# Layer 1's 256x256 products by Strassen's scheme: seven 128x128 block products for two channels and two batches in place of eight

## Chip, cores, metric

The kernel runs on one core of one Trainium2 chip. The metric is device time in microseconds of one execution (with one core, that core's time). A core has five engines that run their own instruction queues [...]: TensorE (matrix products into PSUM; the profile calls it PE and its weight loads PEld), VectorE (DVE), ScalarE (ACT), GpSimd (POOL) and SyncE (SP, which issues most DMAs). A queue is written as its engine with a q: ACTq is ScalarE's queue, in which its DMA issues stand between its computing instructions.

## What is computed

Two layers over an input `x` of 4 x 256 x 256 x 64 (batch, height, width, channel), all in fp32. Layer 0 is a block of layer norm, a Fourier mixing of the plane, a depthwise 3x3 convolution and pointwise products. Layer 1, which this change is about, works along the height alone:

```python
def _L1_conv_ref(x, w_real, w_imag):
    trend = _moving_average(x, KERNEL)
    seasonal = x - trend
    xf = jnp.fft.rfft(seasonal, axis=1)
    xs = xf[:, :M]
    W = w_real + 1j * w_imag
    ys = jnp.einsum('bmnc,cmk->bknc', xs, W)
    ...
    filt = jnp.fft.irfft(yf, n=T, axis=1)
    return trend + filt
```

For a fixed channel all of this is linear in the column of 256 heights, so it is one 256x256 matrix per channel. Layer 1 is then 64 products of a 256x256 matrix with 256 columns for each of 4 batches.

## The kernel before

**Stages.** The kernel builds the 64 matrices of layer 1 early and keeps them in device memory (`m_d`). Layer 0 runs in a long pipeline whose order is written out by hand as lists of operations with due periods, and leaves its result in device memory too (`x2_d`), arranged so that eight channels (CG) of one batch are one contiguous row of 8 KB per partition. Its last lines run until about 3872 us of the span. Then comes layer 1, the last stage, which this change rewrites; nothing else of the kernel is in it.

**Order.** TensorE, VectorE, ScalarE and GpSimd execute in the order in which the program writes their instructions (`in_order`); SyncE's DMAs are placed by the scheduler. Tiles come from pools with a number of buffers for each tag; a new tile waits until all readers of the buffer's earlier tile are done. A DMA also waits for the DMA that used its completion semaphore before; there are eight such semaphores, dealt out in turn to SyncE's and ScalarE's DMAs together.

**Layer 1's loop.** The loop over `c` takes eight channels at a time, the inner loop over `b0` two batches (BH) at a time. `matrix_load` brings the matrices of two channels (CM) as `mt`, 128 partitions x 2 channels x 2 contraction halves `t` x 256 outputs, 512 KB, with eight buffers, that is two groups of eight channels. `x2_load` brings `xc`, the operand of eight channels and two batches, by four DMAs of 1 MB, with one buffer in pool `seq` (the first tile) and three in `seq2`.

**`layer1`.** For each channel and each output half `to` it takes a PSUM bank and issues two matmuls that accumulate over the contraction halves `t`, each with a 128x128 block of `mt` as the weights and 512 columns (two batches x 256) of `xc` as the moving operand. In the trace one such fp32 matmul is two records with a weight load each. The result is evicted with the bias `b_fp[c]`, by VectorE for `to` = 0 (L1518) and by ScalarE for `to` = 1 (L1516), into `oc`, which holds two channels and both batches and has two buffers. When two channels are done, four DMAs of 256 KB, issued by ScalarE (L1523), bring `oc` to the output.

**Banks.** `bank` gives PSUM banks in a ring. Two of the eight banks are given up before layer 0's convolution (`give_back`), which needs them in a pool of its own, and layer 1 keeps to the other six.

Of the kernel before, what the change touches and what calls it, by code (L numbers as in the profile page):

```python
# [11 lines left out]
F32 = mybir.dt.float32  # L12
I32 = mybir.dt.int32
AF = mybir.ActivationFunctionType
ALU = mybir.AluOpType
AX = mybir.AxisListType
PSUM = bass.MemoryType.PSUM
DRAM = bass.MemoryType.DRAM

P = 128  # L20
N = 256
C = 64
# [4 lines left out]
BANKS = 6  # L27
# [109 lines left out]
def conv_seq_kernel(ctx: ExitStack, tc: tile.TileContext, a: dict, tables: bass.AP, out: bass.AP):  # L137
    nc = tc.nc
    x = a["x"]
    B = x.shape[0]  # L140

    consts = ctx.enter_context(tc.tile_pool(name="consts", bufs=1))
    psum = ctx.enter_context(tc.tile_pool(name="psum", bufs=1, space=PSUM))
# [4 lines left out]
    free_banks, taken, lent, busy = list(range(8)), {}, ExitStack(), []  # L148
    pulling = []
    RELEASES = dict(  # L150
        x="xs", m0="b0", m1="b1", z="zs", w="zt", u="uc", s="r1", t0="tt0", t1="tt1", gm="cf0",
# [3 lines left out]
    NEEDS = dict(m0=2, m1=2, u=2, s=2, gm=2, em=2)  # L155
    psum2 = lent.enter_context(tc.tile_pool(name="psum2", bufs=1, space=PSUM))

    def bank(name, keep=True):

        at = free_banks.pop(0)  # L160
        if keep:
            taken[name] = at, busy[-1]
        else:
            free_banks.append(at)
        pool = psum if at < BANKS else psum2
        return pool.tile([P, 512], F32, tag=f"bank{at}", name=name)

    def make_room(op):
# [19 lines left out]
    lent_back = []  # L188

    def give_back():  # L190
        lent_back.append(True)
        for at in range(BANKS, 8):
            if at in free_banks:
                free_banks.remove(at)
# [4 lines left out]
    def row(ap):  # L199
        return ap.rearrange("(o n) -> o n", o=1)  # L200

    def const(shape, name):
        return consts.tile(shape, F32, tag=name, name=name)
# [3 lines left out]
    SW, CG = 16, 8  # L207
# [204 lines left out]
    def prepare(prep):  # L412
# [49 lines left out]
        nc.vector.tensor_copy(w_tegT, ps[:, :C])  # L462
        yield
        ps = bank("ps_wp", False)
        for k in range(2):
            nc.tensor.matmul(
# [1005 lines left out]
        return ops | {"hv": first_half, "hc": between_half, "hm": second_half, "ht": third_half}  # L1472


    CM, CO = 2, 2
    BH = max(1, B // 2)

    b_fp = const([P, C], "b_fp")

    def x2_load(pool, c, b0, bufs):  # L1480
        xc = pool.tile([P, 2, BH, N // SW, CG, SW], F32, tag="xc", name=f"xc_{c}_{b0}", bufs=bufs)
        for b in range(BH):
            for t in range(2):
                nc.sync.dma_start(
                    xc[:, t, b], x2_d[b0 + b, t * P : (t + 1) * P, c // CG]
                )
        return xc

    def matrix_load(pool, c):
        mt = pool.tile([P, CM, 2, N], F32, tag="mt", name=f"mt_{c}", bufs=8)  # L1490
        nc.sync.dma_start(mt, m_d[c : c + CM].rearrange("c p t n -> p c t n"))
        return mt

    def layer1(c, b0, mts, xc, pool):

        nf = BH * N
        oc = None
        for i in range(CG):
            if i % CO == 0:
                oc = pool.tile([P, 2, BH, CO, N], F32, tag="oc", name=f"oc_{c + i}_{b0}", bufs=2)  # L1500
            for to in range(2):
                ps = bank(f"ps_o_{c + i}_{to}_{b0}", False)
                for t in range(2):
                    nc.tensor.matmul(  # L1504
                        ps[:, :nf],
                        mts[i // CM][:, i % CM, t, to * P : (to + 1) * P],
                        xc[:, t, :, :, i, :],
                        start=t == 0,
                        stop=t == 1,
                    )  # L1510
                dst = oc[:, to, :, i % CO, :]
                src = ps[:, :nf].rearrange("p (b n) -> p b n", n=N)

                bias = b_fp[:, c + i : c + i + 1]
                if to:
                    nc.scalar.activation(dst, src, AF.Identity, bias=bias)  # L1516
                else:
                    nc.vector.tensor_scalar(dst, src, bias, None, ALU.add)  # L1518
            if i % CO == CO - 1:
                at = c + i + 1 - CO  # L1520
                for to in range(2):
                    for b in range(BH):
                        nc.scalar.dma_start(  # L1523
                            out[b0 + b, to * P : (to + 1) * P, at : at + CO, :], oc[:, to, b]
                        )

    ET = mybir.EngineType  # L1530
    in_order = tc.manual_schedule(engines={ET.PE, ET.DVE, ET.Activation, ET.Pool})
# [4 lines left out]
    def opened(b):  # L1536

        return (KH * (b + 1) + 2) // 2 + 1

    chunk_at, at = {}, 0  # L1540
    for b in range(B):
        at = max(at, S0 + opened(b) + 2 + LATE)
# [136 lines left out]
    def period(n):  # L1679
        if any(n - k in chunk_at for k in range(7)):  # L1680
            names = FULL if n < B * FWD + 4 else MIXED if n < CONV_FROM else CONV
        else:
            names = SPECTRUM
        joint["on"], joint["whole"] = names is FULL, names is SPECTRUM
        for op, at in names:
            base = n
            if op in PAIRS:
                base = 2 * (n - S0)
            elif op in BACK:
                base = n - S0  # L1690
            elif op in HALF_MATRICES:
                base = (n - S0 - HALF_MATRICES[op]) // 2
            do(op, base + at)

    def starting(n, prep):

        for i, (op, at) in enumerate(FIRST):
            do(op, (3 if op in MATRICES else 2) * n + at)
            if n and i == len(FIRST) // 2:
                next(prep, None)  # L1700

    with in_order, ExitStack() as right:
        with (
            tc.tile_pool(name="fwd", bufs=2, side="left") as fwd,
            tc.tile_pool(name="mix", bufs=2, side="left") as mixing,
        ):
            forward = forward_h(fwd)
            load_group, begin, spectrum = spectral(mixing)
            ops |= forward
            do("fl", 0)  # L1710
            with ExitStack() as early:
                pool = early.enter_context(tc.tile_pool(name="matrices", bufs=2, side="right"))
                prep = early.enter_context(tc.tile_pool(name="prep", bufs=1, side="right"))
                ops |= matrices(pool)
                do("fl", 1)
                nc.sync.dma_start(tab, tables[:, :_L0_END])
                pieces = prepare(prep)
                next(pieces)
                nc.sync.dma_start(b_fp, row(a["b_fp"]).to_broadcast([P, C]))
                for n in range(S0 // 2):  # L1720
                    starting(n, pieces)
                for _ in pieces:
                    pass
                do("yt0", FWD - 1)
                do("yt1", FWD - 1)
                load_group(0)
                for k, names in enumerate(BETWEEN, C - BESIDE - len(BETWEEN)):
                    do("v", k)
                    do("vc", k)
                    do("mt", k - 1)  # L1730
                    for op, at in names:
                        do(op, S0 - 1 + at)
                do("mt", C - BESIDE - 1)
                begin(0)
                ops |= spectrum
                early_end = S0 + 4 * BESIDE + 1
                for n in range(S0, early_end):
                    if n == early_end - 3:
                        give_back()
                    period(n)  # L1740
            lent.close()
            conv = right.enter_context(tc.tile_pool(name="conv", bufs=2, side="right"))
            pairs = right.enter_context(tc.tile_pool(name="pairs", bufs=1, space=PSUM))
            ops |= convolution(conv, pairs)
            for n in range(early_end, S0 + LATE + opened(B - 1) + 2):
                period(n)
        with tc.tile_pool(name="seq", bufs=1, side="left", reuse_waits="tile") as seq:
            mts = [matrix_load(seq, c) for c in range(0, CG, CM)]
            xc = x2_load(seq, 0, 0, 1)
            for n in range(S0 + LATE + opened(B - 1) + 2, END):  # L1750
                period(n)
            right.close()
            with tc.tile_pool(name="seq2", bufs=1, side="right", reuse_waits="tile") as seq2:
                for c in range(0, C, CG):
                    if c:
                        mts = [matrix_load(seq, c + i) for i in range(0, CG, CM)]
                    for b0 in range(0, B, BH):
                        if c or b0:
                            xc = x2_load(seq2, c, b0, 3)
                        layer1(c, b0, mts, xc, seq)  # L1760


# [37 lines left out]
```

## Time and profile before

| what | us |
|---|---|
| three runs | 4324.39, 4318.21, 4323.12; median 4323.12 |
| the profiled execution | 4325.4 |
| its span, first to last instruction | 4323.6 |
| first and last matmul of layer 1, start | 3871.2 and 4317.8 |
| TensorE busy with layer 1's matmuls | 443.3 |
| busy over the whole span: TensorE, VectorE, ScalarE, GpSimd | 4158.0, 3453.4, 2961.5, 3163.4 |

The span is cut into 40 equal slices below, a digit for the busy tenths of each, so that layer 1 is the last four and a bit:

```profile
PE   8999999899999999899999999999998899999999
PEld 4544444345555555455555566666665566654444
DVE  6968999779999998899999878888887799962222
ACT  3338998678888887788888777888885466641111
POOL 6869999688888887788888877888887588840000
PEclk9999999989999999999999999999999999999999
DMA  6664555535454544444444443344433544439995
```

In layer 1 TensorE stays at nine tenths, VectorE falls to two, ScalarE to one and GpSimd to none, while the DMA engines are at nine tenths. The share of busy time over the whole span says nothing of this: it is an average over stages with different limits.

### The profile page before, as it was taken

How to read it: one execution, taken by the hardware profiler on the slowest of the kernel's cores; microseconds unless marked ns; L12 is line 12 of the kernel's file. 1: busy time of each engine (PE TensorE's matmuls, PEld its weight loads, DVE VectorE, ACT ScalarE, POOL GpSimd, SP SyncE). 2: the span in 40 equal slices, each digit the busy share in tenths (PEclk: the TensorE clock that was granted, in tenths of full speed). 3: DMA queues.
4: the chain of work that ended last, by engine and by line, in shares of the span. 5: the costliest groups of instructions: out<-in, count | busy, mean ns of one | idle time of the engine just before them, and what ended most of it. 6: DMA issues, size and time to landing. Idle time of an engine off the chain costs nothing.

```text
span 4323.6 us, 67389 instructions
## 1 busy us (share of the span) xinstructions
PE 4158.0 (96%) x22443; PEld 2315.2 (54%) x22443; DVE 3453.4 (80%) x5234; ACT 2961.5 (68%) x5409; POOL 3163.4 (73%) x3156
## 2 busy tenths in 40 slices
PE   8999999899999999899999999999998899999999
PEld 4544444345555555455555566666665566654444
DVE  6968999779999998899999878888887799962222
ACT  3338998678888887788888777888885466641111
POOL 6869999688888887788888877888887588840000
PEclk9999999989999999999999999999999999999999
DMA  6664555535454544444444443344433544439995
GB/s 190 211 190 142 161 161 162 152 98 137 137 137 137 137 137 124 122 122 138 138 138 129 113 109 109 106 112 112 118 98 91 173 113 118 114 108 358 342 343 228
DMA packets 763906, 655.28 MB, mean 152 GB/s; under 512 B 46413, under 2 KB 657695, under 8 KB 755240
## 3 DMA queue, kind: packets, MB, share of 16 engines
q1 hardware_dynamic: 726696, 583.84, 46.5%
q10 hardware_dynamic: 36864, 67.13, 4.1%
q8 instruction: 180, 2.95, 0.3%
q14 instruction: 166, 1.36, 0.1%
HBM read 364.81 MB, written 286.00 MB: 151 GB/s over the span
## 4 chain that ended last, share of the span: by engine, by line
PE 42%; POOL 6%; DVE 4%; DMA 4%; ACT 3%; issue 1%; SPq 1%; ACTq 0%; POOLq 0%; DVEq 0%
PE ps_o L1504 9%; PE ps_h_c L1166 5%; PE ps_p L750 3%; PE ps_s_c L1041 3%; PE ps_h_c L1180 3%; PE ps_f_c L1283 3%; PE ps_hh_c L1166 2%; PE ps_z L805 2%; PE ps_t_c L1088 2%; PE ps_u L856 2%; PE ps_x L725 2%; PE ps_ft_c L1308 2%; DMA out_dram<-oc 1%; PE ps_zt L823 1%; POOL xb L609 1%
## 5 line engine op out<-in xcount | busy, mean ns | idle before, releaser
L770 DVE TENSOR_TENSOR g<-ps_p,g 128x512 f32<-128x512 f32 x1040 | 702.2, 683 | 127.9 <-ACT g L764 109.7
L781 POOL TENSOR_TENSOR g<-g 128x512 f32<-128x512 f32 (+1 forms) x520 | 677.9, 1315 | 98.5 <-ACT g L775 88.8
L775 ACT ACTIVATE g<-g,b_fc 128x1024 f32<-128x1024 f32 (+1 forms) x520 | 598.3, 1151 | 1.5 <-DVE g L770 1.4
L750 PE MATMUL ps_p<-xs,wp 64*128 64x512 f32 (+1 forms) x2080 | 561.1, 615 | 9.9 <-DVE g L770 2.7
L1166 PE MATMUL ps_h_c<-td,wc_main 128*128 128x256 f32 x2048 | 517.1, 391 | 7.3 <-DVE s_c L1234 0.8
L764 ACT COPY g<-ps_p 128x512 f32<-128x512 f32 (+1 forms) x520 | 298.0, 585 | 268.5 <-PE ps_p L750 101.1
L1504 PE MATMUL ps_o<-xc,mt 128*128 128x512 f32 x1024 | 443.3, 595 | 3.9 <-DVE oc L1518 3.8
L1166 PEld LDWEIGHTS ps_h_c<-td,wc_main 128*128 128x128 f32 x2048 | 370.1, 193 | 122.5 <-ACT zt L833 36.7
L1276 ACT ACTIVATE h_c<-h_c,b_conv 128x1024 f32<-128x1024 f32 x256 | 297.6, 1164 | 140.6 <-DVE h_c L1245 54.1
L1518 DVE TENSOR_SCALAR oc<-ps_o,b_fp 128x512 f32<-128x512 f32 x128 | 93.5, 749 | 351.4 <-DMA out_dram<-oc 196.7
L1516 ACT ACTIVATE oc<-ps_o,b_fp 128x512 f32<-128x512 f32 x128 | 86.2, 686 | 363.0 <-PE ps_o L1504 196.7
L1128 POOL TENSOR_TENSOR td<-tt 128x512 f32<-128x512 f32 x256 | 327.0, 1299 | 10.0
L1504 PEld LDWEIGHTS ps_o<-xc,mt 128*128 128x128 f32 x1024 | 195.3, 191 | 251.2 <-issue 236.0
L609 POOL TENSOR_TENSOR xb<-xt 128x512 f32<-128x512 f32 x224 | 285.4, 1282 | 54.5 <-DVE xt L602 41.1
L750 PEld LDWEIGHTS ps_p<-xs,wp 64*128 64x128 f32 x2080 | 189.3, 186 | 239.6 <-issue 84.7
L805 PE MATMUL ps_z<-g,w_tp 128*64 128x512 f32 x1024 | 288.7, 617 | 24.6 <-POOL g L781 19.9
L725 PEld LDWEIGHTS ps_x<-tab,yb 128*64 128x64 f32 x4064 | 235.0, 138 | 133.3 <-issue 69.2
L1322 DVE TENSOR_TENSOR st<-x_c,ps_ft_c 128x256 f32<-128x256 f32 x512 | 261.8, 602 | 44.4 <-PE ps_ft_c L1308 41.4
L615 PE MATMUL ps_y<-xb,tab 128*64 128x512 f32 x1024 | 273.4, 623 | 23.3 <-POOL xb L609 17.1
L1283 PE MATMUL ps_f_c<-h_c,w_fp 128*64 128x512 f32 x1024 | 266.3, 615 | 15.6 <-ACT h_c L1276 15.5
L1180 PE MATMUL ps_h_c<-td,wc_half 64*128 64x256 f32 (+1 forms) x2048 | 278.6, 396 | 2.4 <-POOL td L1132 1.1
L1041 PE MATMUL ps_s_c<-uc_c,tab 64*128 64x512 f32 x1024 | 259.6, 616 | 15.6 <-DVE uc_c L990 8.7
(201 smaller groups left out, 9559.4 us busy)
## 6 DMA issues: line engine op xcount, KB each, us to landing
y_d<-yt SPq DMA_DIRECT2D x256, 256.0 KB, 3.6
yb<-y_d SPq DMA_DIRECT2D x256, 256.0 KB, 4.0
u_d<-ut SPq DMA_DIRECT2D x256, 256.0 KB, 3.6
x_c<-in_x_dram SPq DMA_DIRECT2D x512, 128.0 KB, 3.6
x_d<-st SPq DMA_DIRECT2D x128, 512.0 KB, 5.1
xc<-x_d SPq DMA_DIRECT2D x64, 1024.0 KB, 8.5
out_dram<-oc ACTq DMA_DIRECT2D x256, 256.0 KB, 5.8
xt<-in_x_dram SPq DMA_DIRECT2D x504, 128.0 KB, 2.5
```

Source lines behind the costliest of these rows:

```text
L609: engine.tensor_tensor(sums[j][:, i], x0, x1, (ALU.add, ALU.subtract)[i])
L750: nc.tensor.matmul(ps[:, :nf], wp[rows, cols], rhs[rows], start=True, stop=r == 1 or not pr["special"],)
L770: nc.vector.tensor_tensor(gt[:, i], re, gt[:, 1], op)
L775: nc.scalar.activation(g, g, AF.Gelu, bias=b_fc[:, half : half + 1])
L781: nc.gpsimd.tensor_tensor(g[:, 0], g[:, 0], g[:, 1], op)
L805: nc.tensor.matmul(ps[r * C : (r + 1) * C, :nf], w_tp, d[:, :nf], start=True, stop=True)
L1041: nc.tensor.matmul(pss[i], tb[i * C : (i + 1) * C], uc[i * C : (i + 1) * C, ::-1, 1 - r, :] if down else uc[i * C : (i + 1) * C, :, r, :], ...
L1128: tt_(new[:, k : k + 3 : 2], a_c, nb_e, op)
L1166: nc.tensor.matmul(product(j, k, par), wc_main[:, par, k, :], td[:, k, slots(j)].rearrange("p j q -> p (j q)"), start=k in (0, 1, 3), stop ...
L1180: nc.tensor.matmul(product(j, k, par)[:, dst.start * Q : dst.stop * Q], wc_half[lo : lo + C, k, :], td[lo : lo + C, k, src].rearrange("p j ...
L1283: nc.tensor.matmul(ps[par * C : (par + 1) * C], w_fp, gs[j][:, :, par, i0 : i0 + 2, :].rearrange("p r j q -> p r (j q)"), start=True, stop ...
L1504: nc.tensor.matmul(ps[:, :nf], mts[i // CM][:, i % CM, t, to * P : (to + 1) * P], xc[:, t, :, :, i, :], start=t == 0, stop=t == 1,)
```

## The change

The 256x256 matrix of a channel is seen as four 128x128 blocks (two contraction halves by two output halves), and the operand as four blocks too: two contraction halves by the two batches. The product of two such 2x2 arrangements takes eight block products by the plain rule; Strassen's scheme (in the form with fifteen sums) takes seven, and sums of blocks before and after.

- `matrix_sums`, once per pair of channels: four sums of matrix blocks by VectorE, into `ms`.
- `operand_sums`, once per pair of channels and pair of batches: four sums of operand blocks by GpSimd, into `x_sums`, which has two buffers.
- `layer1` now handles one pair of channels and one pair of batches. It issues seven products, each of two matmuls (one for each channel) of 128x256 that don't accumulate, into a bank of its own. ScalarE writes product 1 with the bias to `oc`; VectorE adds the other products in seven additions, each of which reads a bank and an earlier part of `oc`. ScalarE then issues the four output DMAs as before. `oc` has four buffers.
- The loop runs over 64 such steps. `ahead` writes the sums of the next step in front of the present step's `layer1`.
- `mt` has four buffers in place of eight, and each is loaded again for the channel eight further on. `xc` has three in place of four.
- Layer 1 gets the two missing banks back (`psum3`), so that the ring has eight.

```diff
-    def layer1(c, b0, mts, xc, pool):
-        nf = BH * N
-        oc = None
-        for i in range(CG):
...
-            for to in range(2):
-                ps = bank(f"ps_o_{c + i}_{to}_{b0}", False)
-                for t in range(2):
-                    nc.tensor.matmul(
-                        ps[:, :nf],
-                        mts[i // CM][:, i % CM, t, to * P : (to + 1) * P],
-                        xc[:, t, :, :, i, :],
-                        start=t == 0,
-                        stop=t == 1,
-                    )
...
+    def matrix_sums(c, mt, pool):
+        ms = pool.tile([P, 4, CM, P], F32, tag=f"ms{c % CG}", name=f"ms_{c}", bufs=1)
...
+        tt = nc.vector.tensor_tensor
+        tt(ms[:, 0], a21, a22, ALU.add)
+        tt(ms[:, 1], ms[:, 0], a11, ALU.subtract)
+        tt(ms[:, 2], a11, a21, ALU.subtract)
+        tt(ms[:, 3], a12, ms[:, 1], ALU.subtract)
+        return ms
+    def operand_sums(c, b0, xc, pool):
+        i = c % CG
+        xs = pool.tile([P, 4, N // SW, CM * SW], F32, tag="x_sums", name=f"x_sums_{c}_{b0}", bufs=2)
...
+        tt = nc.gpsimd.tensor_tensor
+        tt(xs[:, 0], b12, b11, ALU.subtract)
+        tt(xs[:, 1], b22, xs[:, 0], ALU.subtract)
+        tt(xs[:, 2], b22, b12, ALU.subtract)
+        tt(xs[:, 3], b21, xs[:, 1], ALU.subtract)
+        return xs
+    def layer1(c, b0, mt, xc, ms, xs, outs):
...
+        def product(k, a, x):
+            ps = bank(f"ps_o_{name}_{k}", False)
+            for ch in range(CM):
+                nc.tensor.matmul(
+                    ps[:, ch * N : (ch + 1) * N], a[:, ch], x[:, ch], start=True, stop=True
+                )
+            return ps
+        oc = outs.tile([P, 2, BH, CM * N], F32, tag="oc", name=f"oc_{name}", bufs=4)
+        add = lambda dst, x, ps: nc.vector.tensor_tensor(dst, x, ps, ALU.add)
+        p1 = product(1, left(0, 0), right_(0, 0))
+        p6 = product(6, ms[:, 1], sums(1))
+        p2 = product(2, left(1, 0), right_(1, 0))
+        p7 = product(7, ms[:, 2], sums(2))
+        p5 = product(5, ms[:, 0], sums(0))
+        p4 = product(4, left(1, 1), sums(3))
+        p3 = product(3, ms[:, 3], right_(1, 1))
+        for ch in range(CM):
+            cols = slice(ch * N, (ch + 1) * N)
+            nc.scalar.activation(
+                oc[:, 0, 0, cols], p1[:, cols], AF.Identity, bias=b_fp[:, c + ch : c + ch + 1]
+            )
+        add(oc[:, 0, 1], oc[:, 0, 0], p6)
+        add(oc[:, 0, 0], oc[:, 0, 0], p2)
+        add(oc[:, 1, 1], oc[:, 0, 1], p7)
+        add(oc[:, 0, 1], oc[:, 0, 1], p5)
+        add(oc[:, 1, 0], oc[:, 1, 1], p4)
+        add(oc[:, 1, 1], oc[:, 1, 1], p5)
+        add(oc[:, 0, 1], oc[:, 0, 1], p3)
+        for to in range(2):
+            for b in range(BH):
+                nc.scalar.dma_start(
+                    out[b0 + b, to * P : (to + 1) * P, c : c + CM, :],
+                    oc[:, to, b].rearrange("p (c n) -> p c n", c=CM),
+                )
...
+                def ahead(k):
+                    c, b0, at = steps[k]
+                    if (c, b0) not in tiles:
+                        left_one = len(tiles) % 3 == 0
+                        tiles[c, b0] = x2_load(seq if left_one else seq2, c, b0, 1 if left_one else 2)
+                    if b0 == 0:
+                        sums[at] = matrix_sums(at, mt_of[at], seq2)
+                    return operand_sums(at, b0, tiles[c, b0], seq2)
+                xs = ahead(0)
+                for k, (c, b0, at) in enumerate(steps):
+                    if b0 == 0 and at + CG < C:
+                        mt_of[at + CG] = matrix_load(seq, at + CG)
+                    then = ahead(k + 1) if k + 1 < len(steps) else None
+                    layer1(at, b0, mt_of[at], tiles[c, b0], sums[at], xs, seq)
+                    xs = then
```

More of the change, by code (lines that the diff above doesn't have):

```diff
@@ L156, in conv_seq_kernel @@
     psum2 = lent.enter_context(tc.tile_pool(name="psum2", bufs=1, space=PSUM))
+    extra = [psum2]
     def bank(name, keep=True):
@@ L164, in bank @@
             free_banks.append(at)
-        pool = psum if at < BANKS else psum2
+        pool = psum if at < BANKS else extra[-1]
         return pool.tile([P, 512], F32, tag=f"bank{at}", name=name)
@@ L1472, in matrices @@
         return ops | {"hv": first_half, "hc": between_half, "hm": second_half, "ht": third_half}
-    CM, CO = 2, 2
-    BH = max(1, B // 2)
+    CM = 2
+    BH = 2
     b_fp = const([P, C], "b_fp")
@@ L1489, in matrix_load @@
     def matrix_load(pool, c):
-        mt = pool.tile([P, CM, 2, N], F32, tag="mt", name=f"mt_{c}", bufs=8)
+        mt = pool.tile([P, CM, 2, N], F32, tag="mt", name=f"mt_{c}", bufs=4)
         nc.sync.dma_start(mt, m_d[c : c + CM].rearrange("c p t n -> p c t n"))
         return mt
-    def layer1(c, b0, mts, xc, pool):
-        nf = BH * N
-        oc = None
-        for i in range(CG):
-            if i % CO == 0:
-                oc = pool.tile([P, 2, BH, CO, N], F32, tag="oc", name=f"oc_{c + i}_{b0}", bufs=2)
-            for to in range(2):
-                ps = bank(f"ps_o_{c + i}_{to}_{b0}", False)
-                for t in range(2):
-                    nc.tensor.matmul(
-                        ps[:, :nf],
-                        mts[i // CM][:, i % CM, t, to * P : (to + 1) * P],
-                        xc[:, t, :, :, i, :],
-                        start=t == 0,
-                        stop=t == 1,
-                    )
[L1511 to L1525, printed above, removed]
@@ new lines, in matrix_sums @@
+    def matrix_sums(c, mt, pool):
+        ms = pool.tile([P, 4, CM, P], F32, tag=f"ms{c % CG}", name=f"ms_{c}", bufs=1)
+        a11, a12, a21, a22 = (
+            mt[:, :, t, to * P : (to + 1) * P] for to in range(2) for t in range(2)
+        )
[8 more added lines that the diff above has]
+        xs = pool.tile([P, 4, N // SW, CM * SW], F32, tag="x_sums", name=f"x_sums_{c}_{b0}", bufs=2)
+        b11, b12, b21, b22 = (
+            xc[:, t, b, :, i : i + CM, :].rearrange("p s c w -> p s (c w)")
+            for t in range(2)
+            for b in range(BH)
+        )
[5 more added lines that the diff above has]
+        return xs
@@ new lines, in layer1 @@
+    def layer1(c, b0, mt, xc, ms, xs, outs):
+        i = c % CG
+        name = f"{c}_{b0}"
+        left = lambda t, to: mt[:, :, t, to * P : (to + 1) * P]
+        right_ = lambda t, b: xc[:, t, b, :, i : i + CM, :].rearrange("p s c w -> p c s w")
+        sums = lambda k: xs[:, k].rearrange("p s (c w) -> p c s w", c=CM)
+        def product(k, a, x):
[18 more added lines that the diff above has]
+                oc[:, 0, 0, cols], p1[:, cols], AF.Identity, bias=b_fp[:, c + ch : c + ch + 1]
+            )
+        add(oc[:, 0, 1], oc[:, 0, 0], p6)
[10 more added lines that the diff above has]
+                    oc[:, to, b].rearrange("p (c n) -> p c n", c=CM),
+                )
@@ L1752, in conv_seq_kernel @@
             right.close()
[L1753 to L1760, printed above, removed]
+            free_banks.extend(range(BANKS, 8))
+            lent_back.clear()
+            with (
+                tc.tile_pool(name="seq2", bufs=1, side="right", reuse_waits="tile") as seq2,
+                tc.tile_pool(name="psum3", bufs=1, space=PSUM) as psum3,
+            ):
+                extra.append(psum3)
+                steps = [
+                    (c, b0, c + i)
+                    for c in range(0, C, CG)
+                    for b0 in range(0, B, BH)
+                    for i in range(0, CG, CM)
+                ]
+                tiles, sums = {(0, 0): xc}, {}
+                mt_of = dict(zip(range(0, CG, CM), mts))
+                def ahead(k):
[13 more added lines that the diff above has]
+                    xs = then
 _INS = {
```

## The prediction

> **What bounds the kernel now.** I read the page first (engine shares, costliest groups), then the chain of waits from 3860 us on, the windows of the last stage, the tile view of `oc`, and a few moments of the timeline for spacings between instructions. Before the last stage the two programs are the same on every engine (the view that lists instruction order, numbers left out, differs only there), so only layer 1, from 3871 us to the end, can change.
>
> ```profile
> L1504 PE MATMUL ps_o<-xc,mt 128*128 128x512 f32 x1024 | 443.3, 595 | 3.9 <-DVE oc L1518 3.8
> L1518 DVE TENSOR_SCALAR oc<-ps_o,b_fp 128x512 f32<-128x512 f32 x128 | 93.5, 749 | 351.4 <-DMA out_dram<-oc 196.7
> L1516 ACT ACTIVATE oc<-ps_o,b_fp 128x512 f32<-128x512 f32 x128 | 86.2, 686 | 363.0 <-PE ps_o L1504 196.7
> ...
> 3950.63 367.81 PE ps_o L1504 x856
> ...
> 3871.00:3932.00 61.00, 57.23 (x129) 25.02 (x128) 11.95 (x19) 9.69 (x15) 0.00 (x0) 0.95 0.97 362
> 3932.00:4262.00 330.00, 329.87 (x769) 145.64 (x768) 70.52 (x98) 64.84 (x97) 0.00 (x0) 1.00 0.90 340
> ...
> L1523 ACTq DMA_DIRECT2D out_dram<-oc x256: 338/448/2072, 3879.3 to 4319.8; - x128
> ```
>
> The chain is one unbroken piece of TensorE for 368 us. In the windows (TensorE, weight loads, VectorE, ScalarE, GpSimd, clock, DMA share, GB/s) TensorE is busy 329.87 of 330 us, VectorE 21%, GpSimd not at all, DMA 0.90 at 340 GB/s. 769 matmul records in 330 us is 0.429 us each; 1024 records and a slow start make the 447 us from 3871.2 to 4318.5. VectorE and ScalarE only evict, and their waits cost nothing because TensorE has six banks to run into.
>
> These lines give the prices of what is added:
>
> ```profile
> 3847.23 1.89 PE L1166 MATMUL ps_h_c<-td,wc_main 128*128 128x256 f32 x8
> ...
> 3847.03 0.68 DVE L1243 SCALAR_TENSOR_TENSOR h_c<-ps_hh_c,s_c 128x512 f32<-128x512 f32 x1
> 3847.63 0.68 DVE L1244 SCALAR_TENSOR_TENSOR h_c<-ps_hh_c,s_c 128x512 f32<-128x512 f32 x1
> ...
> 3844.97 0.69 DVE L1239 TENSOR_TENSOR ps_hh_c<-h_c,ps_hh_c 128x512 f32<-128x512 f32 x1
> 3845.69 0.70 DVE L1240 TENSOR_TENSOR ps_hh_c<-h_c,ps_hh_c 128x512 f32<-128x512 f32 x1
> ...
> 2467.44 0.70 DVE L1240 TENSOR_TENSOR ps_hh_c<-h_c,ps_hh_c 128x512 f32<-128x512 f32 x1
> 2468.24 0.69 DVE L1242 TENSOR_TENSOR h_c<-ps_hh_c,h_c 128x512 f32<-128x512 f32 x1
> ...
> 3842.98 0.65 ACT L1209 COPY s_c<-ps_h_c 128x256 f32<-128x256 f32 x2 [3.78 <-PE ps_h_c L1180]
> 4119.35 1.85 ACTq L1523 DMA_DIRECT2D out_dram<-oc  x4
> L1128 POOL TENSOR_TENSOR td<-tt 128x512 f32<-128x512 f32 x256 | 327.0, 1299 | 10.0
> L582 DVE TENSOR_TENSOR xb<-xt x256: 674/684/1772, 17.3 to 2391.2; 128x512 f32<-128x512 f32 x128
> ```
>
> The reader should look at starts, not durations: a VectorE instruction follows a free predecessor after 0.60 us, one that waits for VectorE's own last result after 0.72, and one with a further wait beside it after 0.80. Four output DMAs hold ScalarE's queue for 1.85 us (0.34, then 0.45 to 0.48 each, plus 0.04 between).
>
> [...] the spacing of 0.60 is what I use for a chain. [...] eight 128x256 records, each with its own full 128x128 load, take 1.89 us, so 0.216 us apart ((1.89 - 0.38)/7), and the load (0.19 us) is hidden. [...]
>
> **The change, part by part.** One step is now two channels and two batches; there are 64.
>
> TensorE: 8 matmuls of 512 columns (16 records x 0.429 = 6.86 us) become 14 of 256 columns (28 records x 0.216 = 6.05 us). If TensorE stayed the bound, 64 x 0.81 = 52 us would be won.
>
> GpSimd: four sums of 128x512 per step, 4 x 1.30 = 5.2 us, into two `x_sums` buffers. It may start step k+2 when TensorE has used `x_sums` of step k, and has over a step of slack; 5.2 lies under the step. Its 32-element runs are not in the trace: between 1.10 (L1124, strided) and 1.68 (L1125), 4.4 to 6.7 us; I take 5.2. All of it hides beside TensorE.
>
> Matrix sums: four VectorE adds of 256 elements, 0.42 each (L1234), about 1.5 us, in 32 of the 64 steps; placed in front of that step's seven adds. The single `mt` set is reloaded after the fourth product of the b0=2 steps and needed two steps later (some 14 us; the present median to landing is 6.9), and `xc` has three buffers with eight steps between free and needed. I cost these at nothing; a late `mt` would stall VectorE, and with it the stage.
>
> VectorE and ScalarE: this is the part that decides. ScalarE writes product 1 plus bias to `oc`, and VectorE's first add reads it. But on ScalarE's queue these two activations stand behind the four output DMAs of the step before, of which the second waits for that step's seventh add. So there is a ring: last add of step k, three DMA issues, two activations, seven adds of step k+1. Nothing in it overlaps the next turn. Its length:
> - VectorE to ScalarE hand-over: 0.03 (4114.25 to 4114.28 in the timeline).
> - three issues: 0.34 + 0.45 + 0.47 and gaps = 1.38.
> - two activations of 256: the copy pair above takes 0.65; an activation with bias of 512 costs 0.10 more than a copy (686 to 588, L1516 and L764), so 0.72, and 0.08 for both hand-overs.
> - seven adds: three free (0.60), one that waits for itself (0.72, the sixth), two with a wait for itself beside one for TensorE (0.80, the second and fourth), and the last one's duration 0.69: 4.81.
> Sum: 0.03 + 1.38 + 0.08 + 0.72 + 4.81 = 7.02 us a step, against 6.05 for TensorE's 28 records. TensorE, with eight banks, will run about a step ahead and then wait. The matrix sums fall into the 2.2 us in which VectorE waits for ScalarE, so they cost nothing unless one collides with GpSimd (L582's maximum: 1.1 us more).
>
> Sum from the profiled execution: TensorE starts layer 1 at 3871.2 as before (its clock cold for some 2 us, as in the trace); VectorE does eight matrix sums (3.0 us) after its last layer 0 instruction at 3872.5, then the first seven adds, to 3880.4. 63 further turns x 7.02 = 442.3, to 4322.7. From the last result to the end it is 4.4 us as now (4319.15 to 4323.6), so a span of 4327.1, plus 1.8 outside the span (4325.4 - 4323.6) gives 4328.9, and less 2.3 for the distance of the profiled execution to the median (4325.4 - 4323.1): 4326.6 with no disturbance at all.
>
> Disturbances are on the ring now. ScalarE's issues in the timeline of before show 26 of 256 that last over 0.55 us (up to 2.07), 11 us too long together; three quarters stand on the ring: 8. They also waited for an earlier DMA to land: six times 4.1 to 5.2 us in the steady part and five times 1.1 to 2.6 us before 3930, 37 us in all, hidden by the banks. In the new order most DMAs stand over a step from their predecessor on the same semaphore; I take 11, with bounds of 0 and 28 (three quarters of 37). GpSimd collisions: 5 (0 to 30). Total 24, so 4350.6, and **4350** as the forecast.
>
> **The rivals.**
> 1. TensorE stays the bound (not slower). If the ring were shorter than TensorE's 6.05 us, the end would be 3871.2 + 64 x 6.05 + some 8 for cold start and tail, about 4267. For: the windows show 79% of VectorE and all of GpSimd idle. Against: the ring's floor, all issues 0.34, activations 0.65, adds at 0.60, is 6.12 (about 4270). It decides from the ring's length: every 0.1 us is 6.3 us, and with the 24 us of disturbance the kernel is no slower once a turn is under about 6.7, or 7.0 with none. Halfway cases end at 4290 to 4325. Chance of the whole: 0.28 for anything at or under 4332.
> 2. Disturbances in full: the waits for DMA landings as long as ScalarE has them now (28 us on the ring) with GpSimd collisions at their upper bound, or late `mt`, or GpSimd at 1.68 with blocking. For: DMA share already 0.90. Time 4370 to 4420, chance 0.20.
> 3. The ring as priced: 4332 to 4370, chance 0.52.
> DMA as the bound: 145 MB left at the 390 GB/s that the busiest stretch reaches (3900 to 3932) is 372 us; under every case, so it doesn't decide.
>
> **How the numbers follow.** Two tenths of a per cent (8.6 us), about what a measurement can tell, separates the three outcomes at 4314.5 and 4331.8. Case 1 gives 0.13 under the first and 0.15 between; cases 2 and 3 give 0.72 slower. The forecast is 4350; its own case runs from 4332 to 4370. The range 4310 to 4400 leaves out about 0.11 below and 0.08 above.
>
> **What would show it.** Right: in steady windows TensorE at about 0.85 busy with pauses in the fourth product; VectorE's first add of a step released by ScalarE, ScalarE's activation by its own queue (not by TensorE); the DMA of the seventh add 0.03 us after it; a period of 7.0 to 7.4 us. Wrong: TensorE's share above 0.97 and a period of 6.05 (case 1); long gaps of ScalarE at DMA landings, or VectorE's matrix sums waiting for `mt`, or matmuls waiting for GpSimd (case 2). What would make it wrong is a dependency that I overlooked, or adds that are spaced otherwise than in the rows I read.

## The result and the profile after

The changed kernel takes 4356.11 us (median of four runs, 4352.75 to 4356.54), the kernel before 4320.84 in the runs beside it: a ratio of 1.008, with a 95% interval of 1.0066 to 1.0094. The change makes the kernel some 35 us slower. The profiled execution took 4356.44 us, with a span of 4354.7.

First the slices of the changed kernel, for four of the rows shown before:

```profile
PE   7999999899999999899999999999997899988887
...
DVE  6868999789999998899999878888886899968876
...
POOL 6869999688888887788888777888886688856765
...
DMA  6664555535455544445554333344434344458885
```

In layer 1 (the last four slices and a bit) TensorE has gone from nine tenths to eight, and the DMA engines from nine to eight. VectorE and GpSimd, two and nothing before, are at six to eight and five to seven. No engine is full.

The windows of the same two stretches as before, for the changed kernel (columns: TensorE, weight loads, VectorE, ScalarE, GpSimd, clock, DMA share, GB/s):

```profile
3871.00:3932.00 61.00, 52.62 (x224) 43.13 (x223) 42.33 (x72) 5.88 (x14) 35.63 (x29) 0.95 0.92 358
3932.00:4262.00 330.00, 293.88 (x1264) 230.25 (x1263) 261.85 (x409) 37.87 (x91) 232.43 (x181) 1.00 0.86 322
```

TensorE is busy 293.88 of 330 us in place of 329.87, at a granted clock of 1.00 as before, with the DMA share down from 0.90 to 0.86. The stage has lost its bound without getting a new one in any column, which suggests engines that wait for each other in turn. The groups of layer 1 (3871 us to the end) say who waits for whom:

```profile
L1542 DVE TENSOR_TENSOR oc<-oc,ps_o 128x512 f32<-128x512 f32 x448 | 290.5, 684 | 109.6 <-ACT oc L1552 93.7 <-DVE oc L1542 0.5
L1536 PE MATMUL ps_o<-x_sums,ms 128*128 128x256 f32 x768 | 192.3, 386 | 19.6 <-ACT oc L1552 9.8 <-POOL x_sums L1520 5.1 <-issue 2.7
...
L1536 PE MATMUL ps_o<-x_sums,mt 128*128 128x256 f32 x256 | 70.2, 397 | 35.9 <-DVE oc L1542 35.9
...
L1552 ACT ACTIVATE oc<-ps_o,b_fp 128x256 f32<-128x256 f32 x128 | 53.8, 471 | 421.9 <-PE ps_o L1536 200.5 <-DVE ms L1505 119.7 <-DMA out_dram<-oc 71.2
```

VectorE waits for ScalarE, and TensorE waits for both: for ScalarE's release of a bank (product 6 takes the bank of the turn before's product 1) and for VectorE's (product 4 takes that of product 5). The last line has to be read with care. It says that ScalarE's activation waited mostly for TensorE, with ScalarE idle 421.9 us. But the ScalarE rows count only computing instructions, so the DMA issues that fill its queue appear as idle time, and the label goes to the last semaphore event that the activation needed. The timeline shows what held it. Two turns of the changed kernel follow (start, duration, engine, line), first one without matrix sums and then, from 4120.74 on, one with them:

```profile
4080.11 4.79 DVE L1542 TENSOR_TENSOR oc<-oc,ps_o 128x512 f32<-128x512 f32 x7 [2.28 <-ACT oc L1552]
...
4081.67 4.60 ACTq L1564 DMA_DIRECT2D out_dram<-oc  x4
...
4086.37 0.84 ACT L1552 ACTIVATE oc<-ps_o,b_fp 128x256 f32<-128x256 f32 x2 [6.29 <-PE ps_o L1536]
...
4087.24 4.79 DVE L1542 TENSOR_TENSOR oc<-oc,ps_o 128x512 f32<-128x512 f32 x7 [2.34 <-ACT oc L1552]
...
4120.74 0.42 DVE L1503 TENSOR_TENSOR ms<-mt 128x256 f32<-128x256 f32 x1
4120.85 1.46 ACTq L1564 DMA_DIRECT2D out_dram<-oc  x3
...
4121.55 1.52 POOL L1519 TENSOR_TENSOR x_sums<-xc 128x512 f32<-128x512 f32 x1 [1.85 <-PE ps_o L1536]
4121.87 1.49 DVE L1506 TENSOR_TENSOR ms<-mt,ms 128x256 f32<-128x256 f32 x1
...
4122.36 0.84 ACT L1552 ACTIVATE oc<-ps_o,b_fp 128x256 f32<-128x256 f32 x2 [6.51 <-PE ps_o L1536]
...
4123.28 4.77 DVE L1542 TENSOR_TENSOR oc<-oc,ps_o 128x512 f32<-128x512 f32 x7
4123.30 1.10 PE L1536 MATMUL ps_o<-x_sums,ms 128*128 128x256 f32 x4
...
4130.51 4.78 DVE L1542 TENSOR_TENSOR oc<-oc,ps_o 128x512 f32<-128x512 f32 x7
```

In the first turn the seven adds run from 4080.11 to 4084.90. The last three issues follow on ScalarE's queue and end at 4086.27, the activations run from 4086.37 to 4087.21, and the next adds start at 4087.24. VectorE has stood idle for 2.34 us, and the turn is 7.13 us long.

In the second turn the issues end at 4122.31, the activations start 0.05 later and end at 4123.20, and TensorE's product 6 and VectorE's seven adds start within 0.1 of that. The next adds start at 4130.51, 7.23 us later. But here VectorE isn't idle: its matrix sums fill the time from 4120.74 to the adds. Its own work in such a turn, 4.79 us of adds and 2.46 of sums, is 7.25 us, as long as the ring, so that two limits tie in the turns with matrix sums.

### The profile page after: what moved, and what is told of

The parts are those of the page before. It is cut to its first block, busy times and chain, and to the rows that moved or that the text cites. A ratio compares the mean times of both kernels' runs of the same rounds, so it can differ in the third digit from the quotient of the medians.

```text
span 4354.7 us, 70023 instructions
## 1 busy us (share of the span) xinstructions
PE 4131.2 (95%) x23211; PEld 2453.1 (56%) x23211; DVE 3724.7 (86%) x5682; ACT 2929.5 (67%) x5409; POOL 3484.3 (80%) x3412
## 5 line engine op out<-in xcount | busy, mean ns | idle before, releaser
L1542 DVE TENSOR_TENSOR oc<-oc,ps_o 128x512 f32<-128x512 f32 x448 | 290.5, 684 | 109.6 <-ACT oc L1552 93.7
L1552 ACT ACTIVATE oc<-ps_o,b_fp 128x256 f32<-128x256 f32 x128 | 53.8, 471 | 421.9 <-PE ps_o L1536 200.5
L385 POOL TENSOR_TENSOR rstd<-var,minus_half 128x16 f32<-128x16 f32 x74 | 220.7, 2983 | 64.5 <-DVE var L296 64.3
L727 PE MATMUL ps_x<-tab,yb 128*64 128x128 f32 x4064 | 266.6, 275 | 1.5 <-ACT yt L647 0.9
```

The source lines that it names most:

```text
L727: nc.tensor.matmul(ps[r * C : (r + 1) * C, j * N + t * P : j * N + (t + 1) * P], blk[:, t, k, r * C : (r + 1) * C], tb[:, t, :], start=Tru ...
L1542: add = lambda dst, x, ps: nc.vector.tensor_tensor(dst, x, ps, ALU.add)
```

## The experiments

All of them are compared with the kernel before, run beside them. The turn is the time from the first add of a step to that of the next. Turns were worked out from the starts of the single adds in the traces; of the 63, 30 have matrix sums in them.

### Activations ahead of the output DMAs

```diff
+        if before is not None:
+            before()
         add(oc[:, 0, 1], oc[:, 0, 0], p6)
...
-        for to in range(2):
-            for b in range(BH):
-                nc.scalar.dma_start(
+        def write():
+            for to in range(2):
+                for b in range(BH):
+                    nc.scalar.dma_start(
...
+        return write
...
-                    layer1(at, b0, mt_of[at], tiles[c, b0], sums[at], xs, seq)
+                    write = layer1(at, b0, mt_of[at], tiles[c, b0], sums[at], xs, seq, write)
```

> ScalarE writes product 1 of step k+1 before it issues the four output DMAs of step k; no instruction is added or taken away. Ring theory (last add, three issues, two activations, next seven adds: 7.23 us a turn at the median, mean 7.47): the ring is gone. The 32 steps without matrix sums fall to TensorE's 6.05 us, the 32 with them stay at about 7.25, because there VectorE alone has 4.79 us of adds and 2.46 of matrix sums (the last one lengthened to 1.49 us beside GpSimd). Mean 6.65, 63 turns = 419 us from the first add at 3875.1, plus 4.8 and a tail of 5: about 4304, and the waits for DMA landings (18 us in the changed kernel) no longer count. Rival 1, GpSimd's sums set the pace (TensorE is shown waiting for x_sums): nothing changes, 4356. Rival 2, DMA contention sets it: nothing changes, 4350 to 4356.

Measured: 4285.27 us (4281.55 to 4288.97), ratio to the kernel before 0.9916 (0.9899 to 0.9932). The order of two groups of instructions on one queue is worth 71 us, and both rivals fall. All of the gain is in the 33 turns without matrix sums, which fall from 246.4 us together to 172.5; the 30 with them, where VectorE's own work is as long as the ring, go from 223.9 to 229.3. Windows of this kernel, and VectorE's group in it:

```profile
3932.00:4232.00 300.00, 290.43 (x1320) 247.65 (x1320) 278.38 (x426) 40.20 (x96) 242.61 (x190) 1.00 0.99 375
```

```profile
L1542 DVE TENSOR_TENSOR oc<-oc,ps_o 128x512 f32<-128x512 f32 x448 | 291.8, 684 | 34.1 <-ACT oc L1552 11.7 <-PE ps_o L1536 8.4
```

VectorE's wait for ScalarE falls from 93.7 us to 11.7, and TensorE is at 0.97. My 4304 was 19 us too long: I let the steps without matrix sums fall only to TensorE's 6.05 us. They fall to 4.76 at the median, VectorE's own work, because the banks let TensorE get ahead while VectorE does matrix sums. Eight turns in the steady part are 9.41 + 6.47 + 7.41 + 7.23 + 4.69 + 4.70 + 4.76 + 6.04 = 50.7 us, against 8 x 6.05 = 48.4 for TensorE.

### The seventh add's DMA last

```diff
-        for to in range(2):
-            for b in range(BH):
+        for to, b in ((0, 0), (1, 0), (1, 1), (0, 1)):
```

> Only the order of the four output DMAs of a step is changed, so that the part that the seventh add finishes goes last. Ring theory: two of the three issues (0.45 us each) leave the ring, which falls to about 6.2 us; the steps with matrix sums fall no lower than VectorE's own 7.25, so the gain is in the 32 others: mean 6.7 without waits for landings, with them (18 us) about 4325, 4315 to 4335. Rivals (GpSimd or DMA contention set the pace): no change, 4350 to 4356.

Measured: 4324.94 us (4320.13 to 4329.78), ratio to the kernel before 1.001 (1.0001 to 1.0018). The turns without matrix sums have a median of 6.14 us (7.13 in the changed kernel), those with them 7.23 (7.24): two issues less on the ring shorten the first kind by 0.99, and the second kind was at VectorE's own floor already. Two issues of 0.45 us with 0.04 between are 0.98, and nothing but their order differs in this kernel, so the issues stand on the path at their full length.

### Output DMAs issued by SyncE

```diff
-                nc.scalar.dma_start(
+                nc.sync.dma_start(
```

> SyncE issues the output DMAs in place of ScalarE. Ring theory: the ring is gone as when the activations go first, about 4304, if the loads that now stand behind waiting output DMAs in SyncE's queue are early enough; if they come late, VectorE or TensorE waits for mt or xc and the time is 4320 to 4360. Rivals (GpSimd or DMA contention): 4350 to 4356 in any case.

Measured: 4359.3 us (4350.48 to 4362.73), ratio 1.0087 (1.0072 to 1.0102): the branch in which the loads come late. The median turn is 6.34 us, but the mean 7.60. The waits of this kernel between 3932 and 4232 us (us in all, times, longest), of the engines and then of SyncE's queue, and a stretch of that queue:

```profile
POOL x_sums L1520 <- DMA xc<-x_d: 51.6, 9, 8.2
PEld ps_o L1536 <- POOL x_sums L1520: 49.2, 6, 10.4
...
SPq L1564 <- DVE oc L1542: 151.7, 73, 10.8
```

```profile
4109.36 3.34 SPq L1564 DMA_DIRECT2D out_dram<-oc  x4
4112.80 1.24 SPq L1486 DMA_DIRECT2D xc<-x_d  x2
```

The ring is gone (turns of 4.7 us occur again), and the loads now stand behind output DMAs that wait for adds, 151.7 us of the 300: `xc` comes late, GpSimd waits for it and TensorE for GpSimd. Moving the issues off one queue put their wait into another.

### No operand sums after the second step

```diff
-                    return operand_sums(at, b0, tiles[c, b0], seq2)
+                    if k > 1:
+                        return made[k % 2]
+                    made.append(operand_sums(at, b0, tiles[c, b0], seq2))
+                    return made[k]
```

> The operand sums are made for the first two steps only and used again in all later ones, so that GpSimd has nothing to do in layer 1. Ring theory: the ring stays; only the lengthening of the matrix sums beside GpSimd goes (1.07 us in some 24 steps, of which some 0.15 to 0.2 each stands outside the 2.3 us in which VectorE waits anyway): 4 to 6 us less, about 4351. Rival 1, GpSimd sets the pace: TensorE's 6.05 us or VectorE's sum decides, 4270 to 4310. Rival 2, DMA contention: 4356.

Measured: 4345.9 us (4345.23 to 4347.68), ratio 1.0059 (1.0044 to 1.0074). With GpSimd idle through all of layer 1 the time is some 10 us lower (the intervals of the two ratios overlap a little), and the ring is still there: the median turn without matrix sums is 7.13 us, as in the changed kernel. So GpSimd doesn't set the pace. Between the two profiled executions VectorE's lateness accounts for 4.8 us (the table below), and shorter waits in the issues for 7.3 (95.1 against 102.4); my 4 to 6 us had the first alone, and whether the second comes from GpSimd's absence or from scatter isn't shown. The changed kernel's trace also shows TensorE's weight loads waiting for `x_sums` (46 us for the last operand sum alone). They can't wait for GpSimd here, and the turn is the same, so those waits didn't set the pace. What GpSimd does to VectorE shows in the last matrix sum, in the changed kernel and then here (duration min/median/max in ns):

```profile
L1506 DVE TENSOR_TENSOR ms<-mt,ms x32: 413/1486/1494, 3873.3 to 4307.4; 128x256 f32<-128x256 f32 x32
```

```profile
L1506 DVE TENSOR_TENSOR ms<-mt,ms x32: 417/418/422, 3873.5 to 4297.5; 128x256 f32<-128x256 f32 x32
```

### No matrix sums after the first eight channels

```diff
                     if b0 == 0:
-                        sums[at] = matrix_sums(at, mt_of[at], seq2)
+                        sums[at] = matrix_sums(at, mt_of[at], seq2) if at < CG else sums[at - CG]
```

> The changed kernel with the matrix sums made for the first eight channels only and used again for all others. Ring theory: they lie in the time in which VectorE waits for ScalarE's activations, all but some 0.15 us in each of the 28 steps left without them: 4 to 5 us less than the changed kernel, about 4351. Rival, VectorE's work sets the pace: 28 times 2.5 us less, about 4286.

Measured: 4354.15 us (4348.88 to 4356.92), ratio 1.0078 (1.0061 to 1.0095). The 70 us of the rival are excluded; the 5 us of mine are within the scatter of these runs, so their size isn't shown by this one. In the changed kernel the matrix sums are hidden behind the ring: without them the median turn is still 7.12 us.

The same edit was then made in the kernel with the activations first.

> The kernel with the activations ahead of the output DMAs, and the matrix sums made for the first eight channels only and used again for all others. In that kernel each eight steps took 50.7 us where TensorE needs 48.4, because four steps in a row have matrix sums and VectorE is at 7.2 to 9.4 us in them. If that is what is left, TensorE sets the pace here: 63 turns of 6.05 from 3875.5, plus 4.8 and 4.5: span 4266, time about 4266. Rival, DMA (share 0.99 at 375 GB/s there) is the bound: it stays above 4278.

Measured: 4267.47 us (4266.7 to 4270.09), ratio 0.9877 (0.9862 to 0.9891). The windows of this kernel:

```profile
3932.00:4232.00 300.00, 300.00 (x1391) 264.08 (x1391) 228.23 (x350) 41.99 (x100) 248.21 (x200) 1.00 1.01 386
```

Without the ring the same sums are worth some 17 to 18 us. TensorE is busy 300.00 of 300 us, and 1391 records in 300 us are 0.2157 us each. The DMA engines carry 386 GB/s there, so they were not the limit at 375.

### Two versions of the whole computation with the matrix sums spread

```diff
-                    if b0 == 0:
+                    if k < CG // CM:
                         sums[at] = matrix_sums(at, mt_of[at], seq2)
...
+                    g, i = divmod(k + 4, 8)
+                    if i % 2 == 0 and g and g * CG + i < C:
+                        nxt = g * CG + i
+                        sums[nxt] = matrix_sums(nxt, mt_of[nxt], seq2)
```

The buffers change with it (`mt` six, `oc` three, the first `ms` two), and the activations stay first.

> The whole computation. Activations ahead of the output DMAs, and the matrix sums of a group of eight channels spread, one set in every second step instead of four sets in four steps running (mt with six buffers, oc with three, the first ms with two). VectorE then has 2 x 4.75 + 2.5 = 12.0 us in two steps, TensorE 12.1. If the bunching was the loss, TensorE sets the pace: about 4268 (4264 to 4275), faster than both kernels. Rival, DMA is the bound: 4278 to 4285, no change from the kernel with the activations first.

Measured: 4278.81 us (4274.4 to 4280.98), ratio 0.99 (0.9886 to 0.9915). Windows of this kernel, then ScalarE's group in it:

```profile
3871.00:3932.00 61.00, 57.30 (x255) 47.56 (x255) 52.67 (x82) 7.11 (x18) 42.99 (x34) 0.99 1.02 393
3932.00:4232.00 300.00, 297.49 (x1373) 259.95 (x1372) 280.19 (x444) 41.56 (x100) 250.10 (x197) 1.00 1.00 379
```

```profile
L1552 ACT ACTIVATE oc<-ps_o,b_fp 128x256 f32<-128x256 f32 x128 | 53.7, 471 | 341.6 <-DMA out_dram<-oc 198.3 <-PE ps_o L1536 124.5 <-DVE oc L1542 18.8
```

TensorE is at 0.99 in the steady part, so the spreading does what it should there. The time lies above my range of 4264 to 4275. The first eight turns take 58.7 us in place of 48.4, with the DMA share at 1.02, and ScalarE is shown waiting 198 us for output DMAs. But the kernel with the activations first, which has four `oc` buffers, also takes 55.8 us for its first eight turns, and the one without further matrix sums 53.0. So most of the slow start is there with four buffers too; what makes it was not settled. The other 55 turns take 331.4 us here, 6.03 each, and 345.9 with the activations first alone. The interval overlaps with that of the kernel with the activations first (0.9899 to 0.9932): the two are not told apart, while both are faster than the kernel before and than the changed one.

The last run keeps the buffers and changes the order of the steps:

```diff
-                    for b0 in range(0, B, BH)
-                    for i in range(0, CG, CM)
+                    for b0, i in ((0, 0), (0, 2), (2, 0), (0, 4), (2, 2), (0, 6), (2, 4), (2, 6))
```

> The whole computation, activations ahead of the output DMAs, all buffers as in the changed kernel (oc four, mt four). Only the order of the 64 steps is new: within eight channels the two pairs of batches take turns, so that sets of matrix sums fall before steps 0, 1, 3 and 5 of eight in place of 0, 1, 2 and 3. If the bunching is the loss (50.7 us in eight steps against TensorE's 48.4), it goes here without the price of the spread version (oc with three buffers, ScalarE waiting 198 us for output DMAs to land): TensorE sets the pace, 4266 to 4274. Rival, DMA landings are what keeps the spread version from 4267 whatever the buffers: 4276 to 4283.

Measured: 4288.33 us (4277.78 to 4289.46), ratio 0.9923 (0.991 to 0.9937). My 4266 to 4274 was wrong: the time is no better than with the plain order. This order needs the second `xc` tile two steps earlier, and GpSimd waited 18.8 us for it once; the first four turns take 5.76 + 13.20 + 8.07 + 9.39 = 36.4 us, 12 more than 4 x 6.05. The other 59 turns take 366.2 us, against 375.8 with the activations first alone: the order wins some 10 us after the start and loses as much in it. The time lies outside the rival's range (4276 to 4283) as well.

## Why the prediction was right, step by step

The terms of the predicted sum beside the records of the profiled execution, 63 turns, in us:

| term | predicted | measured |
|---|---|---|
| start of the first seven adds | 3880.4 - 4.81 = 3875.6 | 3875.1 |
| seven adds | 63 x 4.81 = 303.0 | 301.7 |
| last add to the waiting issue | 63 x 0.03 = 1.9 | 2.2 |
| three issues, undisturbed | 63 x 1.38 = 86.9 | 63 x 1.336 = 84.2 |
| long issues and waits for landings | 8 + 11 = 19 | 102.4 - 84.2 = 18.2 |
| issue to activations, activations, to the first add | 63 x 0.80 = 50.4 | 4.2 + 52.9 + 2.0 = 59.1 |
| VectorE late because of GpSimd | 5 | 6.8 - 2.0 = 4.8 |
| sum of 63 turns | 466.2 | 470.3 |

(All of it is worked out from the starts and durations of the single instructions. The 2.0 is 63 times the undisturbed hand-over of 0.032 from the activation to the first add; that interval totals 6.8 us. The rest of the distance to 4350 is in the last step of the sum: the profiled execution lies 0.3 us above the median of its runs, where I took 2.3. TensorE's slow start, which I put at some 2 us, is in the granted clock: 0.50 from 3871 to 3873 us in both kernels, then 0.92 to 3875 in the kernel before and 0.96 in the changed one.)

**The ring** is shown, not only fitted. Breaking it takes 71 us away; taking two of the three issues off it takes 0.99 us off a turn that has no matrix sums; and removing GpSimd's or VectorE's other work leaves it at 7.12 to 7.13. The median of all turns is 7.23, inside the 7.0 to 7.4 that I named. What I overlooked is that in the turns with matrix sums VectorE's own 7.25 us is as long as the ring, so that a shorter ring alone wins nothing there.

**TensorE at 6.05 us a step** was right as a floor: 28 x 0.2157 = 6.04 where nothing else holds it (the kernel of 4267.47 us). Its share in the windows is 0.89, not 0.85, because a record's duration (0.38) is longer than the 0.216 between two, so that short pauses are covered; 1264 records x 0.216 = 273 of 330 us, or 0.83. The pauses are before product 4, as I said, but also before product 6, which I had overlooked: its bank is the one that ScalarE's activations release.

**The activations** were the largest mis-sized term on the ring: 0.84 us for the pair, where I took 0.72 from copies plus a difference between two other rows. 63 x 0.12 = 7.6 us, and that is all but 1 us of what the hand-over terms lack.

**The matrix sums** "cost nothing unless one collides with GpSimd": the cost was right and the frequency wrong. I called collisions rare from a median of layer 0 (L582's 684 ns, beside a maximum of 1772). The starts of the single instructions in the kernel before show more: 57 of L582's 256 adds start while a GpSimd TENSOR_TENSOR of 128x512 runs, and each of them ends 0.54 to 0.55 us after that one; 46 of the 57 take 0.79 to 0.87 us. Not every GpSimd instruction does this: the 117 adds that start during L383 (128x16, 2.9 to 3.4 us) take 0.67 to 0.70 us. Here 28 of 32 last sums are lengthened to about 1.49 us, because GpSimd starts its first sum 0.3 us before each time; with GpSimd idle none is (417 to 422 ns). Each of these 28 adds, 0.42 us alone, ends 0.28 to 0.29 us after GpSimd's sum. It cost only 5 us because the four sums together take 2.46 us and VectorE would have waited 2.3 anyway.

**What was luck.** The 5 us for GpSimd were right in size for another reason than mine: I priced a few collisions of 1.1 us each. One early turn lost 1.5 us so, while in the 28 with a lengthened last sum all but 0.2 us or less was hidden. The 11 us for waits for landings were picked between bounds of 0 and 28; of the measured 18.2 about half are such waits and half long issues. Two errors also offset: the activations were 8.7 us short with their hand-overs, the adds and issues 4.0 too long.

**Slips in side sums.** The ring's floor of 6.12 us leaves out the hand-over and one gap; with all terms of the main sum it is 6.19. The limits under which the kernel would be no slower, 6.7 and 7.0 us a turn, use two thresholds; at 4331.8 they are 6.7 and 7.1. Neither moves the forecast.

**The sign for ScalarE** was put wrongly. I said that the activation would be shown released by its own queue; the waits name TensorE and matrix sums instead, and only the timeline shows the queue.

**The rivals.** TensorE as the bound (4267) is what remains when both the ring and the matrix sums go: 4267.47. Disturbances in full did not come: 18.2 us in the issues against the upper bound of 8 + 28 = 36, and no wait of VectorE for `mt`.

## What to carry to other kernels

Count what an engine's queue holds between two dependent instructions: here three DMA issues that waited for VectorE's result, 1.34 us together when undisturbed, delayed the activations written behind them, and as VectorE needed those activations, the lengths added up to a ring that no busy share shows. The sum of the ring's legs from measured spacings gave the time to 6 us, in part by luck, where a balance of engine loads would have promised 52 us of gain. The remedy here was to write what is ready ahead of what must wait; moving the issues to another queue didn't pay, because urgent loads stood there (GpSimd waited 51.6 us for `xc`). Once the ring is gone the next limit is VectorE's bunched matrix sums (2.46 us a set); spread out, they leave TensorE at 0.99 in the steady part.

## What was not expected of the hardware

- In 28 turns a VectorE add with two SBUF inputs started 0.31 to 0.32 us after a GpSimd instruction; it ended 0.28 to 0.29 us after that instruction's end (0.42 us alone, 1.49 so). GpSimd's instruction had itself started 0.02 us after VectorE's third sum, and took about 1.52 in place of 1.27. In one further turn, where VectorE's add started only 0.02 us after GpSimd's, the add was not held. None of the 448 adds with one input in PSUM was lengthened: 673 to 690 ns in the changed kernel, beside the same GpSimd instructions.
- Two activations of 256 columns with bias take 0.84 us, 0.37 from start to start and 0.47 for the last, more than the 0.69 of one of 512 in the kernel before.
- DMA reached 386 GB/s over 300 us (share 1.01) while TensorE was busy for all of them, in the kernel with the activations first and no further matrix sums; the kernel before showed 340 at 0.90.
